# Global attention of a two-block transformer kernel: every unit in two halves with a lead of 13 steps, and three pieces of preparation moved

## The chip, the cores and the metric

One core of a Trainium2 chip runs the kernel. The metric is device time in microseconds (us). TensorE is called PE, VectorE DVE, ScalarE ACT, GpSimd POOL and SyncE SP; SP issues the DMAs.

## The reference

`x` has 2 batches of 2048 tokens with 256 channels, in float32. Two stages follow each other:

```python
x = x + layernorm(attn(layernorm(x)))   # 16 heads of 16, rotary, softmax over all 2048 keys, Wo, bo
x = x + layernorm(ffn(layernorm(x)))    # two layers, each:
#   x = x + local_attention(shift_token(x) @ wqkv) @ wo   (8 heads of 64, window 128, l2norm, xpos)
#   x = x + (a * gelu(g)) @ w2 + b2, with a, g = split(LN(shift_token(x)) @ w1 + b1)
```

The diff touches the first attention, called global here, and the loading of the first weights of the local one.

## The kernel before

**Stages.** Up to 82 us the first batch is normalized and its keys, values and the first queries are projected. From 82 to 1559 us runs the global attention, with the projections of the second batch beside it. After that come the two local layers, which the diff leaves as they are.

**Units and steps.** A unit is (batch, group of 4 heads, block of 512 queries): 32 units in that order. A unit has 16 steps; in each, PE makes 2048 columns of scores (`se`, L543: 50 rows, of which 48 hold three-way split keys and queries and two hold the negated row maximum in a high and a low part), ACT takes four exps of 128x512 (`pe`, L548), and PE multiplies the exps of the step before with the values (`pv`, L517). `spans(u)` cuts the first four units (`HALVED`) into two halves of 256 queries with 8 steps of two key tiles each; the others run whole. In a half, a step's scores are 8 matmuls of 128x256, in a whole unit 4 of 128x512. At the end of a span `collect` (L559 on) copies `pv` to `ov` on ACT and stores it, five DMAs.

**Maxima.** The exact row maximum of a later unit is computed ahead: `row_max` (L436) makes 4 score matmuls per step (`sm`, L412) and DVE reduces each (L452). Since the maximum must be in place before the unit's scores, `finish_max` (L469) follows when a span is complete: negate on DVE (`nm`, L472), split on POOL (`mp`, L477 and L478), then, `DELAY` = 4 steps later, a transpose on PE (`tn`, L481), a copy on ACT (`mt`, L485), a store to DRAM (`md`, L488) and four loads into the two extra rows of the queries (`qs<-md`, L491). The maxima run 13 steps ahead at the start; every fourth step makes two more, until the lead is `TAIL` = 26 steps. So the last 26 steps have no maxima; there the four PSUM banks of pool "sm" are dealt anew as two places of two banks, and the exps are 1024 wide.

**Side work.** `main_loop` writes the order of PE, DVE, ACT and POOL by hand: it takes steps (`s`) and maxima (`m`) in turn, and two lists of generators, `side` (projections of queries and of the second batch, then the closing of blocks: divide by the sums, multiply by Wo, normalize) and `early` (normalizing the second batch's blocks, rotary tables), each of which gives at most one piece in a step. `load_queries` (L398, from `qd` in DRAM) runs when the maxima come near a unit, `load_keys` (L385, from `kd`) one step into each group. `output_weights` (L805) is called at step 3. SP's queue isn't in the hand-written order: the scheduler places its DMAs by its own estimates. After the loop, `last_steps`, three blocks closed by `close_block` (L575) and the pieces left over are merged by their planned times with the local layers; the first local weights are loaded by a strand at -50, with their split on DVE behind the last maxima (L957).

```python
for strand in (s, m, m, s, s, m):   # one step: 3 s, 2 m ... and 2 s, 1 m after the side matmul
    next(strand, None)
if n % EVERY == 0 and lead < TAIL:
    for _ in range(2):
        next(maxima)
    lead += 0.5
side.step(PRODUCTS)
```

Of the kernel before, what the change touches and what calls it, by code (L numbers as in the profile page):

```python
# [20 lines left out]
P = 128  # L21
# [7 lines left out]
NG = 4  # L29
# [18 lines left out]
def tile_sandwich(  # L48
# [369 lines left out]
    def spans(u):  # L418
        return [(0, 2), (2, 4)] if u < HALVED else [(0, 4)]

    def first_max(k, pm):

        q, keys = qs[0], ks[0]
        n = 0
        for t in range(*spans(0)[0]):
            for j in range(0, 4, 2):
                for i in range(2):
                    sc = one("sm", "sm")
                    scores(q, keys, j + i, t, k, sc)
                    nc.vector.tensor_reduce(pm[:, t, j + i, k : k + 1], sc, AX.X, ALU.max)  # L430
                n += 1
                yield 1.2 * n


    reduced, unfinished = [], []

    def row_max():

        due = []
        for u, (b, g, k) in enumerate(units):  # L440
            q, keys = qs[u], ks[g % 2]
            for span in spans(u):
                if (u, span) == (0, spans(0)[0]):
                    continue
                pm = small.tile([P, 4, 4, NBLK], F32, tag="pm", name="pm", bufs=2)
                for t in range(*span):

                    for j, half in [(j, half) for j in (0, 2) for half in (0, 2)]:
                        for kk, i in ((half, 1), (half, 0), (half + 1, 1), (half + 1, 0)):
                            sc = one("sm", "sm")  # L450
                            scores(q, keys, j + i, t, kk, sc)
                            ins = nc.vector.tensor_reduce(  # L452
                                pm[:, t, j + i, kk : kk + 1], sc, AX.X, ALU.max
                            )
                            reduced[:] = [ins.ins]
                            if (kk, i) != (half + 1, 0):
                                yield
                        if (t, j, half) == (span[1] - 1, 2, 2):
                            due = [DELAY, finish_max(u, span, pm)]
                            next(due[1])  # L460
                            unfinished[:] = due[1:]
                        if due and due[0] == 0:
                            for _ in due[1]:
                                pass
                        if due:
                            due[0] -= 1
                        yield
# [32 lines left out]
    TAIL, HALVED, DELAY = 26, 4, 4  # L500


    IN_TURN = {1: (0, 1, 2, 3), 2: (0, 2, 1, 3)}

    def attend():
# [4 lines left out]
        def values(u, span, s, n, pe, pv):  # L510
            b, g, k = units[u]
            w = 512 // n
            for i in range(n):
                for j in range(4):
                    o = (s + i) * 272 + (4 * g + j) * (D1 + 1)
                    c = (4 * i + IN_TURN[n].index(j)) * w
                    nc.tensor.matmul(  # L517
                        pv[SL * j : SL * (j + 1), :w],
                        va[b][:, o : o + SL],
                        pe[c // 1024][:, c % 1024 : c % 1024 + w],  # L520
                        start=(s + i == 0),
                        stop=(s + i == NT - 1),
                    )
            if s + n == NT:
                collect(u, span, pv)

        waiting = None
        for u, (b, g, k) in enumerate(units):
            q, keys = qs[u], ks[g % 2]
            for span in spans(u):  # L530
# [3 lines left out]
                for s in range(0, NT, n):  # L534
                    pe = [t4("pe", tag="pe") for _ in range(2)]

                    m = 2 if u * NT + s >= len(units) * NT - TAIL else 1
                    for c in range(0, 2048, 512 * m):
                        sc = one("se") if m == 1 else two("se")
                        for o in range(c, c + 512 * m, w):  # L540
                            i, j = s + o // (4 * w), IN_TURN[n][o // w % 4]
# [14 lines left out]
                    if (u, s + n) == (len(units) - 1, NT):  # L556
                        values(*waiting)
# [61 lines left out]

    def close_in_pieces(b, k):  # L620
# [31 lines left out]
        for t in range(4):  # L652
            py = one("py", "sm")[:, :C]
# [6 lines left out]
            nc.scalar.copy(y[:, t, :], py)  # L660
            nc.gpsimd.tensor_tensor(y[:, t, :], y[:, t, :], bias_o[0], ALU.add)
# [38 lines left out]
    def first_block(k):  # L700
# [14 lines left out]
        parts0[k] = xh, xl, first_cs if k == 0 else rotary(k, "pe" if k < 2 else "t4")  # L715
# [51 lines left out]

    merged(in_order(strands))
    for _ in finish_max(0, spans(0)[0], pm0):
        pass  # L770
# [3 lines left out]
    lead, EVERY = 13, 4  # L774
    for _ in range(4 * (lead - 8)):
        next(maxima)
# [28 lines left out]
    def output_weights():  # L805
        raw = split_weights("o", wo1, nc.gpsimd, nc.gpsimd.tensor_copy)

        bo = sb.tile([P, C], F32, tag="bo", name="bo")
        bo_raw = t4("bo_raw")[:, :C]
        nc.sync.dma_start(bo_raw, bo1.partition_broadcast(P))  # L810
        bvs = t2("bvs").rearrange("p (c t) -> p c t", c=4)
        for c in range(2):
            nc.vector.tensor_copy(bvs[:, c, :], bqkv[:, 4 + c : 5 + c].to_broadcast([P, P]))
        pb = one("pb", "sm")
        for c in range(2):
            nc.tensor.matmul(pb[:, :C], bvs[:, c, :], raw[:, c, :], start=(c == 0), stop=(c == 1))
        nc.vector.tensor_tensor(bo, bo_raw, pb[:, :C], ALU.add)
        return bo
# [25 lines left out]
    def main_loop(lead, loaded):  # L844
        normalized = {}
        early = Pieces(
            *[normalized_block(1, k, normalized) for k in range(NBLK)],
            *[rotary_tables(l) for l in range(DEPTH)],
        )
        side = Pieces(  # L850
            *[project_qk(0, k, 0, *parts0[k]) for k in range(2, NBLK)],
            *[project(1, k, normalized) for k in range(NBLK)],
        )
        for n in range(1, len(units) * NT - TAIL + 1):
# [5 lines left out]
            if n % EVERY == 0 and lead < TAIL:  # L860
                for _ in range(2):
                    next(maxima)
                lead += 0.5
            side.step(PRODUCTS)
            for strand in (s, m, s):
                next(strand, None)
            early.step(OTHER, WAIT)
            side.step(OTHER, WAIT)
            if n % NT == 0:
                b, g, k = units[n // NT - 1]  # L870
                if g == NG - 1 and (b, k) < (1, 1):
                    side.add(close_in_pieces(b, k))
# [7 lines left out]
            if (n + lead + 3) // NT >= loaded and loaded < len(units):  # L880
                load_queries(loaded)
                loaded += 1
            if n == 3:
                bias_o.append(output_weights())
        assert next(maxima, 0) == 0 and early.kind is None
        return side

    in_turn = {mybir.EngineType.PE}
    with tc.manual_schedule(engines=ENGINES):
        side = main_loop(lead, loaded)  # L890
# [4 lines left out]
    def last_steps():  # L895
        for n in range(TAIL):
# [7 lines left out]
    strands = [(LAST - TAIL * STEP, last_steps())]  # L904
    for i, place in enumerate((LAST + CLOSE, LAST + CLOSE - NT * STEP, -46.0)):
        strands.append((place, close_block(B - 1, NBLK - 1 - i, "t4" if i > 0 else "pe")))

    def last_pieces():
        while side.kind is not None:
            side.step(PRODUCTS, OTHER, WAIT)  # L910
            yield 0.0

    strands.append((-50.0, last_pieces()))
# [8 lines left out]
    zero = sb.tile([1, C], F32, tag="zero", name="zero")  # L922
    mid_d = {
# [21 lines left out]

    def raw_columns(src, nk, n, step, tag):

        sv = src.rearrange("(k p) o -> p k o", p=P)
        for o in range(0, n, step):
            m = min(step, n - o)  # L950
            raw = t4("raw", tag=tag)[:, : nk * m].rearrange("p (k o) -> p k o", k=nk)
            nc.sync.dma_start(raw, sv[:, :, o : o + m])
            yield o, m, raw

    weights = {}

    def load_attn_weights(l, pace, tag, copy):  # L957
        tiles = [large_v(0, f"attnh_{l}", F32R), large(0, f"attnl_{l}", F32R)]
        n = 2 * 3 * INNER
        wq = [t[:, :n].rearrange("p (k o) -> p k o", k=2) for t in tiles]  # L960
        wo = [t[:, n : n + 4 * C].rearrange("p (k o) -> p k o", k=4) for t in tiles]
        weights["attn", l] = wq, wo
        if l == 0:
            nc.gpsimd.memset(zero, 0.0)
        t = 0.0

        for n in (1, 0, 2):
            cols = slice(n * INNER, (n + 1) * INNER)
            for _, _, raw in raw_columns(wqkv2[l][:, cols], 2, INNER, INNER, tag):
                yield t + 4.0  # L970
                with tc.issue_after(reduced[-1]):
                    split(wq[0][:, :, cols], wq[1][:, :, cols], raw, copy=copy)
                t += pace
                yield t
        for _, _, raw in raw_columns(wo2[l], 4, C, C, tag):
            yield t + 4.0
            with tc.issue_after(reduced[-1]):
                split(wo[0], wo[1], raw, copy=copy)
# [62 lines left out]
    WEIGHTS_FROM = -50.0  # L1041
# [496 lines left out]
    strands.append((WEIGHTS_FROM, load_attn_weights(0, 2.0, "t4", nc.vector.tensor_copy)))  # L1538
    ffn_weights_from = LAST + 20.0
    for l in range(DEPTH):  # L1540
# [14 lines left out]
        if l + 1 < DEPTH:  # L1555
            strands.append((start + 55.0, load_attn_weights(l + 1, 20.0, "pe", nc.scalar.copy)))
# [108 lines left out]
```

## Time and profile before

| | |
|---|---|
| runs | 2873.26, 2874.59, 2887.58 us; median 2874.59 |
| profiled run | 2879.28 us, of which the span is 2877.5 us |
| mean granted PE clock | 0.973 of full speed |
| busy: PE, DVE, ACT, POOL | 2707.5, 2317.9, 1898.2, 1288.1 us |
| DMA | 163.72 MB, 57 GB/s on the mean |

A line of the groups reads: line, engine, operation, out<-in, shape, count, then busy time and mean ns of one, then the idle time of the engine just before such instructions and what ended it. A line of a timeline reads: start, duration, engine, line, operation, count, and in brackets the idle time before it and its releaser. The chain of waits is followed back from the end; each piece has its start and its length. `PEclk` gives the granted clock in 40 slices of the span, in tenths; 9 is 90% or more.

### The profile page before, as it was taken

The page shows a single profiled execution, that of the slowest core. Times are in us where ns is not written, and L with a number is a line of the kernel's source. Part 1 is how long each engine was busy: PE and PEld are TensorE (multiplying, and loading weights), DVE is VectorE, ACT ScalarE, POOL GpSimd, SP SyncE. Part 2 cuts the span into 40 slices and gives each one's busy share as a digit, 9 for nine tenths or more (in the row PEclk, how much of TensorE's full clock was granted, in tenths as well). Part 3 has the DMA queues.
Part 4 walks back from the last instruction along what each step waited for, and adds up shares of the span by engine and source line. Part 5 has one row for each costly group of instructions (what it writes and reads, how often), then busy time and mean ns, then how long its engine had stood idle before and what let it go on. Part 6 is the DMA issues. An engine that isn't in the chain of part 4 may idle for free.

```text
span 2877.5 us, 50638 instructions
## 1 busy us (share of the span) xinstructions
PE 2707.5 (94%) x18496; PEld 1627.8 (57%) x18496; DVE 2317.9 (81%) x5006; ACT 1898.2 (66%) x4015; POOL 1288.1 (45%) x1244
## 2 busy tenths in 40 slices
PE   7989999999999999999988899999999899999998
PEld 5545433333333333333334777777788678787787
DVE  6878888889999999999975788887454788887565
ACT  3456677777878777788876576676443667676432
POOL 4253212131121312200036688886455678786465
PEclk8789999999999999999999999999999999999999
DMA  7033211111111111100022110111232111111232
GB/s 218 20 92 112 67 30 43 42 46 53 40 34 51 52 38 47 54 9 17 18 91 84 52 50 31 32 47 44 81 108 59 54 42 39 34 44 41 82 106 71
DMA packets 154721, 163.72 MB, mean 57 GB/s; under 512 B 32716, under 2 KB 117880, under 8 KB 154472
## 3 DMA queue, kind: packets, MB, share of 16 engines
q1 hardware_dynamic: 154472, 160.48, 18.7%
q8 instruction: 147, 2.41, 0.4%
q14 instruction: 102, 0.84, 0.1%
HBM read 98.89 MB, written 49.04 MB: 51 GB/s over the span
## 4 chain that ended last, share of the span: by engine, by line
PE 74%; DVE 11%; ACT 8%; POOL 3%; issue 2%; DMA 2%; SPq 0%; POOLq 0%; DVEq 0%; ACTq 0%
PE pv L517 17%; PE se L543 15%; ACT pe L548 5%; PE sm L412 4%; PE s L1240 4%; PE o L1307 3%; DVE pm L452 3%; PE w L1289 3%; PE p L172 3%; PE p L176 2%; PE p L174 2%; PE pag L172 2%; PE pag L174 2%; PE pag L176 2%; PE t L1214 2%
## 5 line engine op out<-in xcount | busy, mean ns | idle before, releaser
L452 DVE TENSOR_REDUCE pm<-sm 128x1 f32<-128x512 f32 x2016 | 1247.7, 683 | 119.9 <-PE sm L412 92.0
L548 ACT ACTIVATE pe<-se 128x512 f32<-128x512 f32 (+1 forms) x1996 | 1060.3, 614 | 349.1 <-PE sm L412 258.1
L412 PE MATMUL sm<-ks,qs 48*128 48x512 f32 x2048 | 778.0, 462 | 21.9 <-DMA qs<-qd 8.3
L543 PE MATMUL se<-qs,ks 50*128 50x512 f32 (+1 forms) x2304 | 743.1, 421 | 53.4 <-ACT pe L548 49.8
L543 PEld LDWEIGHTS se<-qs,ks 50*128 50x128 f32 x2304 | 361.3, 190 | 619.6 <-ACT pe L548 536.5
L517 PE MATMUL pv<-pe,va 128*32 128x512 f32 (+1 forms) x4608 | 557.3, 566 | 0.0
L412 PEld LDWEIGHTS sm<-ks,qs 48*128 48x128 f32 x2048 | 355.3, 190 | 62.2 <-DVE pm L452 32.2
L1279 POOL TENSOR_TENSOR e<-e,rs 128x1024 f32<-128x1024 f32 (+1 forms) x128 | 254.2, 1986 | 86.6 <-DVE rs L1275 86.6
L1264 ACT ACTIVATE e<-e,mns 128x256 f32<-128x256 f32 (+1 forms) x512 | 253.4, 498 | 15.4 <-DVE mns L1252 11.7
L477 POOL CAST mp<-nm 128x16 fp32r<-128x16 f32 (+1 forms) x35 | 6.9, 198 | 523.7 <-DVE nm L472 268.6
L95 POOL TENSOR_TENSOR rn<-ss,mhalf 128x8 f32<-128x8 f32 x128 | 214.9, 1679 | 10.6
L1166 ACT ACTIVATE sq<-p 128x512 f32<-128x512 f32 x128 | 76.6, 598 | 173.7 <-PE p L176 171.0
L1252 DVE CUSTOM_DVE_ANT_0 e<-s,mask 128x256 f32<-128x256 f32 (+1 forms) x512 | 181.5, 410 | 10.8 <-PE s L1240 9.4
L1189 POOL TENSOR_TENSOR ra<-qk,tab 128x512 f32<-128x512 f32 x128 | 171.8, 1354 | 18.2 <-DVE qk L1181 18.2
L517 PEld LDWEIGHTS pv<-pe,va 128*32 128x32 f32 x4608 | 99.0, 110 | 134.9 <-issue 107.9
L172 PE MATMUL p<-attnh,xTh 128*128 128x512 f32 x384 | 169.1, 440 | 2.9 <-ACT kT L1227 2.5
L1199 DVE TENSOR_TENSOR rb<-qk,tab 128x256 f32<-128x256 f32 x256 | 164.8, 684 | 0.4 <-PE pv L517 0.2
L1296 ACT COPY eT<-w 128x1024 f32<-128x1024 f32 (+1 forms) x128 | 126.0, 984 | 49.9 <-PE w L1289 47.9
L333 POOL TENSOR_TENSOR rotation<-raw,cs 128x512 f32<-128x512 f32 x40 | 50.4, 1282 | 232.7 <-ACT raw L329 232.7
L174 PE MATMUL p<-attnl,xTh 128*128 128x512 f32 x384 | 153.4, 400 | 0.0
L1240 PE MATMUL s<-kT,qT 64*128 64x256 f32 (+1 forms) x1024 | 142.8, 397 | 11.2 <-ACT qT L1224 3.1
L176 PE MATMUL p<-attnh,xTl 128*128 128x512 f32 x384 | 153.2, 399 | 0.0
(201 smaller groups left out, 4864.4 us busy)
## 6 DMA issues: line engine op xcount, KB each, us to landing
xb<-mid SPq DMA_DIRECT2D x32, 512.0 KB
qs<-qd SPq DMA_DIRECT2D x192, 64.0 KB
kd<-parts SPq DMA_DIRECT2D x16, 512.0 KB
ks<-kd SPq DMA_DIRECT2D x64, 128.0 KB
qd<-parts SPq DMA_DIRECT2D x16, 512.0 KB
tab<-rotary SPq DMA_DIRECT2D x64, 128.0 KB
mid<-xb SPq DMA_DIRECT2D x16, 512.0 KB
xt<-in_x SPq DMA_DIRECT2D x12, 512.0 KB
```

Source lines behind the costliest of these rows:

```text
L95: nc.gpsimd.tensor_tensor(dst, src, mhalf[:, :n], ALU.pow)
L172: nc.tensor.matmul(out, lh, rh, start=first, stop=False)
L174: nc.tensor.matmul(out, lh, rl, start=False, stop=False)
L176: nc.tensor.matmul(out, ll, rh, start=False, stop=last)
L412: return nc.tensor.matmul(out, q[rows, j // 2, t * P : (t + 1) * P], keys[rows, k, j // 2, :], start=True, stop=True)
L452: ins = nc.vector.tensor_reduce(pm[:, t, j + i, kk : kk + 1], sc, AX.X, ALU.max)
L517: nc.tensor.matmul(pv[SL * j : SL * (j + 1), :w], va[b][:, o : o + SL], pe[c // 1024][:, c % 1024 : c % 1024 + w], start=(s + i == 0), sto ...
L543: nc.tensor.matmul(sc[:, o - c : o - c + w], keys[rows, i // 4, j // 2, i % 4 * P : (i % 4 + 1) * P], q[rows, j // 2, span[0] * P : span[1 ...
L548: nc.scalar.activation(pe[c // 1024][:, c % 1024 : c % 1024 + 512 * m], sc, AF.Exp, scale=1.0 / math.sqrt(D1),)
L1240: nc.tensor.matmul(get(f"s{hf}", two)[:, o + lo : o + 2 * P], at["qT"][own, a * P : (a + 1) * P], kT[own, windows, a, :], start=True, stop ...
L1264: nc.scalar.activation(e4(h // 4)[:, h % 4, lo:], e4(h // 4)[:, h % 4, lo:], AF.Exp, bias=mns[:, h : h + 1], scale=-1.0, accum_out=rs[:, h ...
L1279: nc.gpsimd.tensor_tensor(e4(hf)[:, :, lo:], e4(hf)[:, :, lo:], rs[:, hs].rearrange("p (a o) -> p a o", o=1).to_broadcast([P, 4, 2 * P - lo]),
```

## The change

Every unit of the global attention is now cut in two halves (`SPANS`), so each runs 8-step halves, with the matmuls of 128x256 that the first four units had; transposes, negations and output copies rise from 36 to 64, the stores of maxima with them, and the loads of maxima from 144 to 256. The lead of the maxima is 13 steps throughout (`LEAD`); no extra maxima are made, the main loop has 499 steps for 486, and the tail 13 for 26. A strand `third_queries` projects the third block's queries ahead of the main loop. `output_weights` becomes a generator among the early pieces, with its copies on POOL and its loads ahead of four waits. The first local weights are loaded and split by POOL in pieces from step 452 on (`load_attn_weights` through `in_steps`), for DVE at the transition. Of the last batch's blocks, two (for three) are closed by `close_block`; the block (1, 1) is closed in pieces from a list of its own, `last`. `issue_after` and `reduced` are gone.

```diff
-    def spans(u):
-        return [(0, 2), (2, 4)] if u < HALVED else [(0, 4)]
+    SPANS = [(0, 2), (2, 4)]
...
-            for span in spans(u):
-                if (u, span) == (0, spans(0)[0]):
+            for span in SPANS:
+                if (u, span) == (0, SPANS[0]):
...
-    TAIL, HALVED, DELAY = 26, 4, 4
-    IN_TURN = {1: (0, 1, 2, 3), 2: (0, 2, 1, 3)}
+    LEAD, DELAY = 13, 4
+    IN_TURN = (0, 2, 1, 3)
...
-                    m = 2 if u * NT + s >= len(units) * NT - TAIL else 1
+                    m = 2 if 2 * u * NT + span[0] // 2 * NT + s >= 2 * (len(units) * NT - LEAD) else 1
...
+                            i, j = s + o // (4 * w), IN_TURN[o // w % 4]
...
-            py = one("py", "sm")[:, :C]
+            py = one("py", "sm" if "sm" in pools else "one")[:, :C]
+            live.append(py)
...
             nc.scalar.copy(y[:, t, :], py)
+            live.pop()
...
-        parts0[k] = xh, xl, first_cs if k == 0 else rotary(k, "pe" if k < 2 else "t4")
...
+    def third_queries():
+        n = 0.0
+        for kind in project_qk(0, 2, 0, *parts0[2]):
+            if kind == OTHER:
+                n += 1.0
+                yield n
+    strands.append((101.0, third_queries()))
...
-    lead, EVERY = 13, 4
-    for _ in range(4 * (lead - 8)):
+    for _ in range(4 * (LEAD - 8)):
...
     def output_weights():
-        raw = split_weights("o", wo1, nc.gpsimd, nc.gpsimd.tensor_copy)
+        t = t4("raw")
...
+        nc.sync.dma_start(bo_raw, bo1.partition_broadcast(P))
+        nc.sync.dma_start(raw, wo1.rearrange("(k p) o -> p k o", p=P))
+        for _ in range(4):
+            yield WAIT
...
+        split(*parts, raw, nc.gpsimd, nc.gpsimd.tensor_copy)
+        w1parts["o"] = parts
...
-        bo_raw = t4("bo_raw")[:, :C]
-        nc.sync.dma_start(bo_raw, bo1.partition_broadcast(P))
-        bvs = t2("bvs").rearrange("p (c t) -> p c t", c=4)
         for c in range(2):
-            nc.vector.tensor_copy(bvs[:, c, :], bqkv[:, 4 + c : 5 + c].to_broadcast([P, P]))
+            nc.gpsimd.tensor_copy(bvs[:, c, :], bqkv[:, 4 + c : 5 + c].to_broadcast([P, P]))
+        for _ in range(3):
+            yield WAIT
         pb = one("pb", "sm")
         for c in range(2):
             nc.tensor.matmul(pb[:, :C], bvs[:, c, :], raw[:, c, :], start=(c == 0), stop=(c == 1))
+        yield OTHER
         nc.vector.tensor_tensor(bo, bo_raw, pb[:, :C], ALU.add)
-        return bo
+        bias_o.append(bo)
...
+    def load_attn_weights(l, pace, tag, eng, copy):
...
+        for n in (1, 0, 2):
+            cols = slice(n * INNER, (n + 1) * INNER)
+            for _, _, raw in raw_columns(wqkv2[l][:, cols], 2, INNER, INNER, tag):
+                yield t + 4.0
+                split(wq[0][:, :, cols], wq[1][:, :, cols], raw, eng, copy)
+                t += pace
+                yield t
+        for _, _, raw in raw_columns(wo2[l], 4, C, C, tag):
+            yield t + 4.0
+            split(wo[0], wo[1], raw, eng, copy)
...
+    def in_steps(generator, waits):
+        for _ in generator:
+            for _ in range(waits):
+                yield WAIT
...
-    def main_loop(lead, loaded):
+    def main_loop(loaded):
         normalized = {}
         early = Pieces(
             *[normalized_block(1, k, normalized) for k in range(NBLK)],
+            output_weights(),
             *[rotary_tables(l) for l in range(DEPTH)],
         )
         side = Pieces(
-            *[project_qk(0, k, 0, *parts0[k]) for k in range(2, NBLK)],
+            project_qk(0, 3, 0, *parts0[3]),
             *[project(1, k, normalized) for k in range(NBLK)],
         )
-        for n in range(1, len(units) * NT - TAIL + 1):
+        last = Pieces()
+        for n in range(1, len(units) * NT - LEAD + 1):
             s, m = steps, maxima
             for strand in (s, m, m, s, s, m):
                 next(strand, None)
-            if n % EVERY == 0 and lead < TAIL:
-                for _ in range(2):
-                    next(maxima)
-                lead += 0.5
             side.step(PRODUCTS)
+            last.step(PRODUCTS)
             for strand in (s, m, s):
                 next(strand, None)
             early.step(OTHER, WAIT)
             side.step(OTHER, WAIT)
+            last.step(OTHER, WAIT)
             if n % NT == 0:
                 b, g, k = units[n // NT - 1]
-                if g == NG - 1 and (b, k) < (1, 1):
-                    side.add(close_in_pieces(b, k))
+                if g == NG - 1 and (b, k) < (1, 2):
+                    (side if (b, k) < (1, 1) else last).add(close_in_pieces(b, k))
             if n % (4 * NT) == 1 and n > 1:
                 i = n // (4 * NT) + 1
...
                     assert side.kind is None
                 if i < B * NG:
                     load_keys(i // NG, i % NG)
-            if (n + lead + 3) // NT >= loaded and loaded < len(units):
+            if (n + LEAD + 3) // NT >= loaded and loaded < len(units):
                 load_queries(loaded)
                 loaded += 1
-            if n == 3:
-                bias_o.append(output_weights())
+            if n == (len(units) - NBLK) * NT + 4:
+                early.add(
+                    in_steps(load_attn_weights(0, 0.0, "t4", nc.gpsimd, nc.gpsimd.tensor_copy), 2)
+                )
+        while live:
+            for pieces in (side, last):
+                if pieces.kind is not None:
+                    pieces.step(PRODUCTS, OTHER, WAIT)
         assert next(maxima, 0) == 0 and early.kind is None
-        return side
+        return side, last
...
     def last_steps():
-        for n in range(TAIL):
+        for n in range(LEAD):
...
-    strands = [(LAST - TAIL * STEP, last_steps())]
-    for i, place in enumerate((LAST + CLOSE, LAST + CLOSE - NT * STEP, -46.0)):
+    strands = [(LAST - LEAD * STEP, last_steps())]
+    for i, place in enumerate((LAST + CLOSE, LAST + CLOSE - NT * STEP)):
         strands.append((place, close_block(B - 1, NBLK - 1 - i, "t4" if i > 0 else "pe")))
-    def last_pieces():
-        while side.kind is not None:
-            side.step(PRODUCTS, OTHER, WAIT)
-            yield 0.0
-    strands.append((-50.0, last_pieces()))
+    def last_pieces(pieces):
+        n = 0.0
+        while pieces.kind is not None:
+            pieces.step(PRODUCTS, OTHER, WAIT)
+            n += STEP / 2
+            yield n
+    for pieces in left:
+        strands.append((LAST - LEAD * STEP, last_pieces(pieces)))
...
-    strands.append((WEIGHTS_FROM, load_attn_weights(0, 2.0, "t4", nc.vector.tensor_copy)))
```

## What is predicted

> **What bounds the kernel now.** I read the page first (span, busy shares, groups), then the timeline of ScalarE, because one step of the global attention is four exps of 128x512 and the time from the first exp of one step to that of the next is the price of a step; then the chain of waits around the odd steps; then SyncE's queue.
>
> ```profile
> span 2877.5 us, 50638 instructions
> ...
> PEclk8789999999999999999999999999999999999999
> ...
> L452 DVE TENSOR_REDUCE pm<-sm 128x1 f32<-128x512 f32 x2016 | 1247.7, 683 | 119.9 <-PE sm L412 92.0
> ...
> L543 PE MATMUL se<-qs,ks 50*128 50x512 f32 (+1 forms) x2304 | 743.1, 421 | 53.4 <-ACT pe L548 49.8
> ```
>
> PE is busy 94% of the span and hardly waits in the global attention, which the diff rewrites (82 to 1559 us; on every engine the instructions behind it stand in the same order in both kernels). A step also owes four row-max reduces, 4 x 0.683 = 2.73 us of VectorE, so VectorE is nearly as full as PE.
>
> ```profile
> 281.60 2.07 ACT L548 ACTIVATE pe<-se 128x512 f32<-128x512 f32 x4 [0.63 <-PE se L543]
> 284.36 2.06 ACT L548 ACTIVATE pe<-se 128x512 f32<-128x512 f32 x4 [0.70 <-PE se L543]
> 287.13 2.07 ACT L548 ACTIVATE pe<-se 128x512 f32<-128x512 f32 x4 [0.70 <-PE se L543]
> ...
> 289.90 1.57 ACT L548 ACTIVATE pe<-se 128x512 f32<-128x512 f32 x3 [0.44 <-PE se L543]
> ...
> 293.84 2.07 ACT L548 ACTIVATE pe<-se 128x512 f32<-128x512 f32 x4 [1.07 <-PE sm L412]
> ```
>
> Ordinary steps with a projection matmul take 2.77 us here (281.60 to 287.13 to 289.90); the step from 289.90 takes 3.94, since it carries the two extra maxima of every fourth step. The same view gives 2.69 for a halved step without projection (197.59 to 200.28) and 2.61 for a whole one (1303.72 to 1306.33). A transpose of maxima adds 0.43 to a step with a projection (499.20 to 502.40 is 3.20) and 0.21 to one without (2.82 against 2.61).
>
> Three steps are far off, where a load is late. Here the chain of waits around the third:
>
> ```profile
> 315.19 0.25 ACT mt L485
> 315.44 0.02 issue
> 315.45 3.62 DMA md<-mt
> 319.07 0.02 issue
> 319.09 0.02 SPq L491
> 319.11 0.03 issue
> 319.14 1.30 DMA qs<-md
> 320.44 0.14 issue
> 320.58 0.47 PE se L543
> ```
>
> PE stands for 2.22 us until the maxima are back from DRAM, and the table by windows shows what follows: the granted clock from 322 to 336 us is 0.51.
>
> ```profile
> 206.00:226.00 20.00, 19.84 (x114) 10.63 (x116) 10.31 (x16) 7.62 (x15) 6.78 (x8) 0.50 0.29 77
> 282.00:293.00 11.00, 10.79 (x112) 6.51 (x112) 10.16 (x18) 8.23 (x17) 1.40 (x3) 1.00 0.36 102
> 322.00:336.00 14.00, 14.00 (x60) 5.23 (x59) 7.45 (x12) 7.18 (x15) 1.96 (x2) 0.51 0.14 36
> ```
>
> The columns end with clock, DMA share and GB/s. At half clock a step takes 4.9 us instead of 2.77, so 43% of the throttled time is lost; the throttled stretches after stalls last 3.4 to 20 us, which makes 1.5 to 9 us each, 4.5 as a middle.
>
> **The change, part by part.** The sum is made against the profiled run, 2879.3 us (1.8 beyond its span, 4.7 above the median of the runs).
>
> *Lead constant, early steps (5 to 113; 369.7 us before).* The 26 extra pairs of maxima go: 1.2 to 1.45 us each, some 34 us. The three stalls as they stood go with their half clock: (11.13 - 2.77) + (8.5 and three of 4.9, less 4 x 2.77) + (6.4, 4.5, 4.9, 4.9, less 4 x 2.77), some 30. Built up afresh from the listing of the changed kernel's instructions: 90 steps with a projection at 2.77, 13 of those with a transpose at 3.20, 5 plain ones at 2.69 and one plain with a transpose at 2.90 make 307.3, which is **-62.4**.
>
> *Steps 114 to 193* (223.4 before): 58 x 2.77, 8 x 3.20, 12 x 2.69, 2 x 2.90 = 224.4, **+1.0**; the projections end earlier, but these units are halved now.
>
> *Steps 194 to 486* (782.5 before): 208 x 2.69, 29 x 2.90, 49 x 2.77, 7 x 3.20 = 801.7, **+19.2**. This is the price of halving where PE waits for ScalarE: the scores become 4096 matmuls of 128x256 for 512 and 1792 of 128x512, the first exp of a step needs two of them, and there are 28 more each of transposes, negated maxima and output copies. Bounds: +6, if each of the 38 halves there gets the 0.35 that a whole unit's switch saves (two steps in 2.69 + 2.18 for 5.22), or more if a matmul of 256 costs over half of one of 512. I take 19.2, from the halved steps that the trace has.
>
> *Third block's queries ahead:* 12 matmuls more before the loop, at half clock (55.9 to 103.7 us) some +2.6; the output-weight matmuls leave step 3, -2.0; fewer extra maxima there, -1.4: **-1**. *Weights in pieces on POOL:* POOL is 45% busy; casting and subtracting a 128x1024 piece, by the 1.28 us of its 128x512 products, is about 5 us, and POOL's other duty here, splitting the negated maxima (0.2 us), has four steps, 11 us, before the transpose. Hidden; if POOL were behind by more, each late transpose would cost what a late chain costs. *Last steps:* VectorE's casts leave steps 486 to 489, but 13 more steps keep their maxima: **+2.8** up to step 499, and **+2** for one more transpose and its copies in the 13 remaining steps (0 to 5).
>
> *The chain of maxima, now due at once.* In the trace, from the first exp of a step with a transpose to maxima landed takes 5.04 us: copy after the last exp, the store issued at about 2.2 us, its landing and the first load at 3.6, the loads 0.29 apart, 1.44 for the last transfers. Before, a lead that rises to 26 steps against units of 16 leaves 5 steps and more for it. In the new kernel half h begins two steps after its transpose, each time: the maxima are needed 5.37 us after that first exp beside projections (0.33 of slack) and 4.97 in plain steps, where the later loads miss their matmuls by about 0.43: 31 x 0.43 = **+13.3**. When a score matmul waits for it, the whole PE queue stands behind (maxima, values, projections), and with it the exps and reduces.
>
> A page speaks against the change here: the Trainium skill, "DMA: Bandwidth & Descriptors", in the section on what happens when a kernel issues a DMA, gives about 2.0 us fixed for each, most of it waiting for the write's receipt. By that, store and load would take 4.0 us for the measured 1.40 and 1.30 (501.36 to 502.76, and the chain above), every half would wait some 1.3 us longer, and the sum would be some 70 us higher; the trace has the shorter times, so they stand.
>
> So far -62.4 + 1.0 + 19.2 - 1 + 2.8 + 2 + 13.3 = -25, or 2854.
>
> *What is in SyncE's queue ahead of the chain.* The trace shows the chain late by 1 us and more for about a quarter of its 36 transposes, behind other traffic:
>
> ```profile
> 765.99 0.38 SPq L638 DMA_DIRECT2D rb<-rsum  x1
> 766.41 0.47 SPq L640 DMA_DIRECT2D xt<-in_x  x1
> 766.99 0.44 SPq L488 DMA_DIRECT2D md<-mt  x1
> 771.77 1.16 SPq L491 DMA_DIRECT2D qs<-md  x4
> ```
>
> Behind two loads of 512 KB the 16 KB store needs 4.78 us instead of 1.40. Before, nothing waited for it. The order of SyncE's queue is the scheduler's, and in the new kernel's listing these stand before the store, or between store and loads: both stores of the last queries at the third half (POOL issues the second 11.9 us after the projection's last step: late by 4.3); the rotary tables' 512 KB loads and the key reload around the sixth to ninth half (some 5); queries, keys and tables of the second batch at four halves (3.5 and 3 x 1.8); the closing of blocks (stores waiting for POOL's last add, the loads of sums, 5.0 us after their store, and key and weight loads) at halves 32 (2.3), 38 (5.9), 47 (weights, 2 MB at the 190 GB/s of the case above, 8), 48 (3.7), 59 (1.8) and 61 (3.3). Sum 43. Eight of these exceed 2.2 us, so the half clock may follow: 8 x 4.5 at 6 in 10, 22. Together **+65**, with 0 and 115 as ends: the scheduler's order is fixed, but whether the waits in it last is not known until it runs. That a stall costs its clock rests on the 2.22 us gap above.
>
> The Trainium skill, "TensorE: Matmul & The Clock Gate", "Why this matters for your kernels", would keep full speed up to gaps of about 3 us; by that, one of the eight (2.3) would go without its clock, 2.7 us less. The 2.22 us gap of this trace decides against it.
>
> 2854 + 65 = 2919 in the profiled run's terms, less 4.7: **2915**.
>
> **The rivals.** *First, faster:* the chain gets through in time, since the queue is in order but what stands ahead may be done by then. Price: the 65 is not paid, 2850. It decides at the store's landing: as long as the first load of maxima is issued within 3.9 us of the first exp of the transposing step, the 62 us stay gained. For it: three quarters of the chains of before were on time. Against it: those late ones were under lighter traffic (1079 transfers, now 1359). *Second, about the same:* only part of the delays occur, some 15 to 40 us, 2860 to 2889. *Third, much slower:* the early steps keep a hump (VectorE, at 2.73 of 2.77 us, doesn't catch up after a stall) or the reloads hold SyncE's queue longer than listed: the 34 us of maxima or 50 more of delays come back, 2960 and more. *Fourth, within the first:* halved plain steps take 2.61 like whole ones, 208 x 0.08 = 17 less: 2833.
>
> **How the numbers follow.** Forecast with its band 2889 to 2960: 0.48. First and fourth: 0.25. Second: 0.15. Third: 0.12. The range 2840 to 2970 leaves out the fourth and half of the third. 0.5%, 14 us, is about what a measurement can tell from no change, so faster is below 2860 and slower above 2889: 0.25, 0.15, 0.60. The forecast's own range is 2889 to 2960.
>
> **What would show it.** Right: steps of 2.77 without humps up to step 113; gaps on PE ended by the load of maxima at the named halves, with the clock at 0.5 behind some; halved plain steps at 2.69. Wrong: the chain's loads on time at all those halves (first rival), steps of 2.61 or of 2.8 and more in the late units, or POOL ending the wait for the transpose.

## The result, and the profile after

The changed kernel is slower: 2980.64 us in the median (2967.81 to 2989.69) for 2876.98, a ratio of 1.035 with an interval of 1.029 to 1.041. The forecast was 2915 with a range of 2840 to 2970: the right side, but the time lies above the range, and the loss is 104 us for a forecast 40. The profiled run took 2989.4 us, 110 more than that of the kernel before; times and stretches read from traces below are of the profiled runs.

The page of the changed kernel first: its span, the granted clock by fortieths, and the groups of the reduces and of the scores.

```profile
span 2987.6 us, 62908 instructions
...
PEclk8799899999999899999999999999999999999999
...
L451 DVE TENSOR_REDUCE pm<-sm 128x1 f32<-128x512 f32 x2016 | 1247.1, 681 | 255.8 <-PE sm L412 222.6
...
L541 PE MATMUL se<-qs,ks 50*128 50x256 f32 x4096 | 779.6, 314 | 137.4 <-DMA qs<-md 80.1
```

Two readings. The reduces cost what they did (1247 us), but VectorE now stands for 256 us before them, for 120 before. And the scores, which waited mostly for exps (49.8 of 53.4 us), now wait mostly for the load of the maxima. The view of the waits gives the number (us in total, times, longest):

```profile
PE se L541 <- DMA qs<-md: 80.1, 45, 9.5
PE se L541 <- ACT pe L546: 54.6, 207, 0.5
```

Seventeen of these waits are 1 us or longer and make 70 of the 80 us. The chain of waits around the second longest, before step 377 (dots stand for rows left out):

```profile
1245.34 1.68 SPq L848
...
1248.10 0.47 SPq L848
...
1248.67 6.67 DMA md<-mt
...
1255.40 1.27 DMA qs<-md
1256.68 0.14 issue
1256.81 1.08 PE se L541 x2
```

SyncE issues four 512 KB loads of the first local weights (L848), then the 8 KB store of the maxima (L486). ScalarE had copied the maxima by 1245.34; the store leaves at 1248.67, and 6.67 us later it has landed and the loads can go. PE stands for 8.6 us and then works at half clock, from 1251.72 to 1261.96: its two score matmuls of 256 columns take 1.08 us. Another place, by SyncE's timeline before step 65:

```profile
302.88 3.08 SPq L811 DMA_DIRECT2D rotary<-tab  x2
306.05 2.13 SPq L392 DMA_DIRECT2D ks<-kd  x4
308.28 0.37 SPq L486 DMA_DIRECT2D md<-mt  x1
311.14 1.14 SPq L489 DMA_DIRECT2D qs<-md  x4
```

Here the store has been ready since 299.7 and stands behind two stores of rotary tables that wait for POOL, and behind four key loads. The table by windows shows the clock after two of the waits (the last three columns are clock, DMA share and GB/s):

```profile
314.00:331.00 17.00, 17.00 (x101) 9.34 (x101) 9.77 (x17) 8.98 (x18) 3.82 (x6) 0.50 0.26 73
555.00:569.00 14.00, 13.86 (x88) 7.78 (x86) 7.97 (x14) 6.58 (x14) 0.40 (x2) 0.51 0.12 30
```

The first follows the wait of 9.5 us before step 65, the second one of only 2.35 us. Over the main loop (110 to 1597 us) the trace has 18 stretches at half clock of 3.4 to 27.3 us, 160 us in all.

By stretches of steps, from first exp to first exp, in us:

| steps | before | changed | lead 16, tables late (below) |
|---|---|---|---|
| start of step 1 | 82.1 | 86.1 | 84.3 |
| 1 to 4 | 26.0 | 23.9 | 27.7 |
| 5 to 113 | 369.7 | 352.9 | 312.1 |
| 114 to 193 | 223.4 | 245.5 | 224.5 |
| 194 to 486 | 782.5 | 871.6 | 797.9 |
| 487 to 510 | 69.0 | 81.0 | 72.2 |

### The profile page after: what moved, and what is told of

Read it like the earlier page. It is cut to its first block, busy times and chain, and to the rows that moved or that the text cites. A ratio compares the mean times of both kernels' runs of the same rounds, so it can differ in the third digit from the quotient of the medians.

```text
span 2987.6 us, 62908 instructions
## 1 busy us (share of the span) xinstructions
PE 2750.3 (92%) x23900; PEld 1932.4 (65%) x23900; DVE 2310.6 (77%) x5018; ACT 1905.7 (64%) x4099; POOL 1316.1 (44%) x1318
## 4 chain that ended last, share of the span: by engine, by line
PE 65%; DVE 10%; ACT 8%; DMA 7%; POOL 5%; issue 3%; SPq 1%; POOLq 0%; ACTq 0%; DVEq 0%
PE pv L515 14%; PE se L541 11%; PE sm L412 6%; ACT pe L546 5%; PE s L1273 3%; DVE pm L451 3%; PE o L1340 3%; PE w L1322 3%; PE p L172 3%; DMA md<-mt 3%; PE p L174 2%; PE p L176 2%; DMA qs<-md 2%; PE pag L172 2%; PE pag L174 2%
## 5 line engine op out<-in xcount | busy, mean ns | idle before, releaser
L541 PE MATMUL se<-qs,ks 50*128 50x256 f32 x4096 | 779.6, 314 | 137.4 <-DMA qs<-md 80.1
L541 PEld LDWEIGHTS se<-qs,ks 50*128 50x128 f32 x4096 | 525.1, 195 | 467.0 <-ACT pe L546 299.7
L515 PE MATMUL pv<-pe,va 128*32 128x256 f32 x8192 | 575.5, 400 | 1.0 <-ACT pe L546 0.3
L412 PEld LDWEIGHTS sm<-ks,qs 48*128 48x128 f32 x2048 | 392.6, 194 | 24.2 <-DVE pm L429 14.5
L475 POOL CAST mp<-nm 128x8 fp32r<-128x8 f32 x62 | 11.9, 193 | 783.5 <-DVE nm L470 678.4
L515 PEld LDWEIGHTS pv<-pe,va 128*32 128x32 f32 x8192 | 219.2, 112 | 176.5 <-issue 28.3
L1273 PE MATMUL s<-kT,qT 64*128 64x256 f32 (+1 forms) x1024 | 142.8, 397 | 10.2 <-ACT eT L1329 3.3
L1340 PE MATMUL o<-eT,v 128*64 128x128 f32 x1984 | 138.6, 282 | 12.1 <-ACT eT L1329 12.1
```

Source lines behind the costliest of these rows:

```text
L412: return nc.tensor.matmul(out, q[rows, j // 2, t * P : (t + 1) * P], keys[rows, k, j // 2, :], start=True, stop=True)
L515: nc.tensor.matmul(pv[SL * j : SL * (j + 1), :w], va[b][:, o : o + SL], pe[c // 1024][:, c % 1024 : c % 1024 + w], start=(s + i == 0), sto ...
L541: nc.tensor.matmul(sc[:, o - c : o - c + w], keys[rows, i // 4, j // 2, i % 4 * P : (i % 4 + 1) * P], q[rows, j // 2, span[0] * P : span[1 ...
L1273: nc.tensor.matmul(get(f"s{hf}", two)[:, o + lo : o + 2 * P], at["qT"][own, a * P : (a + 1) * P], kT[own, windows, a, :], start=True, stop ...
L1340: nc.tensor.matmul(ps("o")[D2 * par : D2 * par + D2, o : o + P], made[b, i - 1 + j]["v"][:, h * D2 : (h + 1) * D2], at[f"eT{hf}"][:, (2 * ...
```

## The experiments

Theory A: the sum without delays holds, and what was missing in it is the chain store, load of maxima, late behind SyncE's queue, with half clock after it. Theory B: halves are dear in themselves. Theory C: SyncE's many issues have become the bound. Ratios are to the kernel before, measured beside each.

**More slack for the chain.**

```diff
-    LEAD, DELAY = 13, 4
+    LEAD, DELAY = 16, 4
```

> The changed kernel with a lead of 16 steps for 13, so that the transpose of each half's maxima comes three steps (some 8 us) earlier against the half that needs it. Theory A (the chain store, load of maxima is late behind SyncE's queue, and half clock follows): the gaps on PE of 1 to 8.6 us that end with a load of maxima vanish, at most the two longest (9.5 and 8.6 us) leave 1 us or so, the clock stays at full speed in the main loop after step 5, and the time falls by 110 to 135 us, to 2845 to 2875. Theory B (halves themselves are dear: twice the matmuls, twice the transposes, more transfers): 2940 and more. Theory C (SyncE has become the bound by its number of issues): the late loads come back at other halves, 2920 and more.

Measured 2861.67, ratio 0.993 (0.990 to 0.995): 119 us less than the changed kernel by three steps of lead, with the same halves, transposes and transfers. One wait for maxima is left:

```profile
PE se L541 <- ACT pe L546: 61.6, 225, 0.6
PE tn L479 <- DVE pm L451: 7.9, 35, 0.7
PE se L541 <- DMA qs<-md: 6.0, 1, 6.0
```

B and C fall as causes of the loss: the halves and the number of transfers stay, the loss goes.

**One step of slack** (`LEAD` 14).

> The changed kernel with a lead of 14 for 13: one step (2.7 us) more for the chain. Theory A: each gap of the changed kernel that ended with a load of maxima is 2.7 us shorter or gone, so of 17 gaps over 1 us nine are left with some 34 us, and their half clock; with 2850 as the sum without delays, 2900 to 2930. Theory C (late loads reappear wherever the lead puts the halves): no such order, 2940 and more.

Measured 2888.72, ratio 1.0025 (1.000 to 1.005): below the range that A gave. Five waits with 25.4 us stay where subtraction had said nine with 34. Three of them shrank by 0 to 2 us (9.5, 8.4 and 6.2 us, for 9.5, 8.6 and 8.2 with a lead of 13), not by 2.7, while others of 6 to 7 us are gone whole. An earlier store may find another queue ahead of it; that wasn't shown here. One step undoes 92 of the 119 us.

**The transpose two steps earlier** (`DELAY` 2, `LEAD` 13).

> The changed kernel with 2 steps for 4 between the negation and the transpose of the maxima, the lead left at 13: the chain starts two steps (5.4 us) earlier. Theory A: the gaps shrink by about 5.4 us each, six of them are left with 0.7 to 4 us, the half clock goes in some ten places, and the time is 2875 to 2915. Theory B: 2950 and more. A second price could show: POOL, in its bursts of projection work, splits the negated maxima too late for the earlier transpose, and PE waits for the split in the first 190 steps.

Measured 2878.46, ratio 0.9975 (0.995 to 1.000). Three waits for maxima, 13.8 us, are left; the two long ones are shorter by 0.9 and 3.3 us, not by 5.4 (8.6 for 9.5 before step 65, 4.9 for 8.2 before step 353). The second price shows, though not where it was expected: the transpose waits for POOL's split three times, 4.77 us at 800 us and 1.28 at 1067, behind POOL's other work.

```profile
PE se L541 <- DMA qs<-md: 13.8, 3, 8.6
...
PE tn L479 <- POOL mp L476: 6.5, 3, 4.8
```

**Halving alone** (the kernel before with `HALVED` 30, the lead still rising to 26).

> The kernel before with all but the last two units in halves (HALVED 30 for 4), the lead still rising to 26: halving alone, with slack for the chain. Theory A: 8 to 25 us above the kernel before, 2885 to 2900, with no gap on PE that ends with a load of maxima but the one before step 65. Theory B: 2960 and more. If plain halved steps gained at the switch what whole ones do, the same time as before, 2877.

Measured 2903.46, ratio 1.0071 (1.005 to 1.009): some 20 us, which is the +1.0 and +19.2 of the prediction (steps 114 to 193 take 226.0, 194 to 486 take 801.2). In its trace no score waits for a load of maxima.

**The third block's queries ahead, alone.**

```diff
+    strands.append((101.0, third_queries()))
...
-            *[project_qk(0, k, 0, *parts0[k]) for k in range(2, NBLK)],
+            project_qk(0, 3, 0, *parts0[3]),
```

> The kernel before with the third block's queries projected ahead of the main loop and nothing else. Expected by the sum of the prediction: the gap of 5.5 us before step 19 goes with its half clock (8 to 10 us), the projection at half clock ahead of the loop costs 2.6, so 2867 to 2873. Rival: the gap only moves to the next queries that are loaded late, 2875 to 2880.

Measured 2870.46, ratio 0.996 (0.994 to 0.998), some 11 us less. The gaps before steps 19 and 33 are both gone; the one before step 65 is now 4.0 us.

**The store of maxima on ScalarE's queue.**

```diff
-        nc.sync.dma_start(md.rearrange("t j s q -> (t j s) q"), mt.bitcast(F32))
+        nc.scalar.dma_start(md.rearrange("t j s q -> (t j s) q"), mt.bitcast(F32))
```

> The changed kernel with the store of the maxima issued by ScalarE right behind its copy, the loads left on SyncE. If the place of the store in SyncE's queue makes the chain late, the halves whose store stood behind other transfers (steps 16, 64, 256, 384, 472) gain 2.4 to 4.6 us each, some 15 to 25 in all with their clock, and those whose loads stood behind (steps 304, 488) stay as they are: 2935 to 2965. If the traffic itself (2 MB of weights before step 376, 1 MB before 472) delays the small transfers, those two stay too: 2955 to 2980.

Measured 2958.29, ratio 1.0285 (1.025 to 1.032): 22 us less than the changed kernel, a time that lies in both ranges and so doesn't decide. Waits for maxima fall from 80.1 to 59.1 us. Those at steps 304 and 488 stay (6.2 to 6.3 and 6.1 to 5.9 us), as expected of halves whose loads stood behind. The waits at steps 16, 256, 384 and 472 are shorter by 1.4 to 1.7 us, less than the 2.4 to 4.6 expected; the one at 288 grows from 1.1 to 4.7; and ScalarE now stands for 5.9 us itself before step 65, with the store of the maxima in its queue. Order and traffic aren't told apart by it: before step 377, where the wait falls from 8.6 to 2.4 us, three of the four weight loads now follow the loads of maxima.

**Lead 16 with the rotary tables at step 200.**

```diff
+            if n == 200:
+                early.add(*[rotary_tables(l) for l in range(DEPTH)])
```

> The kernel with a lead of 16, and the rotary tables of the local layers put among the early pieces at step 200 for step 25 or so, when no projections are left. If the one gap that the lead of 16 has (6.0 us at 291 us, with 10.2 us at half clock) comes from the stores of those tables ahead of the key reload and the store of maxima in SyncE's queue, it goes: 8 to 11 us less than with the lead of 16 alone, 2850 to 2855 where that one has 2862. If the key reload itself makes the chain late, the gap stays: 2860.

Measured 2849.58, ratio 0.990 (0.987 to 0.993), some 28 us below the kernel before and the fastest of all: the gap at 291 us is gone, and no score waits for maxima at all.

**The same with a lead of 18.**

> The same with a lead of 18: two steps more of slack, 2 steps more of maxima before the loop and 2 fewer at the end. If the lead of 16 with the tables moved has no late chain, more slack brings nothing: within 4 us of it. If chains are still late there, another 3 to 8 us less.

Measured 2860.09, ratio 0.9935 (0.991 to 0.996): slower by 10, where 4 was the bound. No chain is late; what grows are steps 1 to 4 (32.8 for 27.7) and 487 to 510 (76.7 for 72.2). More slack than the chain needs costs.

**With a lead of 15.**

> The kernel with the rotary tables late and a lead of 15 for 16: one step less of maxima ahead of the loop, one step less of slack. If 8 us of slack are what the chain needs: one or two late chains come back, 2855 to 2870. If 5.4 us do now that the tables are out of the way: 2845 to 2851.

Measured 2878.73, ratio 0.998 (0.996 to 1.001), above both ranges. The two longest waits are 8.6 and 5.1 us. SyncE's timeline around the first:

```profile
735.28 1.36 SPq L796 DMA_DIRECT2D tab<-in_xpos_s  x1
746.03 0.37 SPq L811 DMA_DIRECT2D rotary<-tab  x1
746.49 0.52 SPq L486 DMA_DIRECT2D md<-mt  x1
749.41 1.15 SPq L489 DMA_DIRECT2D qs<-md  x4
```

The store of a rotary table waits for POOL until 746.03, and the maxima, copied since 734, behind it. With a lead of 16 the store of the same half leaves 0.5 us after its copy (720.15, copied at 719.66). So the order at one place decides, and one step of lead moves the order.

**The price of a stall by itself.** Spare copies on ScalarE ahead of one step in 16 halves of the kernel with lead 16 and the tables late, three in one kernel and six in the other.

```diff
+                    if 12 <= u < 28 and span == SPANS[0] and s == 8:
+                        for _ in range(3):      # 6 in the second
+                            nc.scalar.copy(pe[0][:, 0:512], va[b][:, 0:512])
```

> The kernel with a lead of 16 and the rotary tables late, which has no late chain, and on purpose three spare copies of 128x512 on ScalarE ahead of one step in the middle of 16 halves (units 12 to 27), some 1.6 us each time, so that PE stands for about 1.2 us with nothing else changed. If a short gap costs itself alone: 16 x 1.2 = 19 us or less, 2864 to 2870. If it is followed by half clock, as after the gaps of 1.0 to 1.7 us in the changed kernel: throttled stretches of 3.4 to 6.8 us after most of them, 1.5 to 3 us each more, 2885 to 2915.

> The same with six copies, some 3.2 us each time, so that PE stands for about 2.8 us. Gap alone: 16 x 2.8 = 45, 2890 to 2897. With half clock after each (7 to 10 us throttled, 43% of what of it PE works): 3 us or so more each, 2925 to 2955.

Measured 2908.62 (ratio 1.009, 1.006 to 1.012) and 2985.58 (1.033, 1.027 to 1.040): the first in its upper range, the second above both. These times don't decide, since late chains came back in both (two waits, 11.4 and 13.4 us, before steps 225 and 353 as with a lead of 15), in the first a gap of 9.0 us at 1554 too. The stalled halves themselves do. One of the 16 falls into a stretch that was at half clock already. At the other 15, with three copies, PE stands for 0.95 to 1.4 us, and 5 are followed by half clock, for 3.4 to 6.8 us; the 13 steps around a stall (the copies come in the fourth) are longer by 1.1 us or so than in the kernel without copies (but for one next to a late chain), and by 2.3 to 3.6 at four of the five; at the fifth the kernel without copies is at half clock itself. With six copies PE stands for 2.9 to 3.35 us, all 15 are followed by 3.4 to 17.1 us, and the 13 steps are longer by 7.6 us in the median (4.1 to 9.7). Copies, then the steps behind them, on ScalarE's timeline of the second:

```profile
1075.13 3.86 ACT L538 COPY pe<-va 128x512 f32<-128x512 f32 x6
1079.03 2.07 ACT L549 ACTIVATE pe<-se 128x512 f32<-128x512 f32 x4
1083.10 2.08 ACT L549 ACTIVATE pe<-se 128x512 f32<-128x512 f32 x4 [2.00 <-PE sm L412]
1087.23 2.08 ACT L549 ACTIVATE pe<-se 128x512 f32<-128x512 f32 x4 [2.06 <-PE sm L412]
1091.37 2.08 ACT L549 ACTIVATE pe<-se 128x512 f32<-128x512 f32 x4 [2.06 <-PE sm L412]
```

Steps of 2.68 us are 4.13 for as long as the clock is 0.50, as its table by windows says:

```profile
1073.00:1079.00 6.00, 3.07 (x35) 1.79 (x33) 4.37 (x7) 5.77 (x11) 0.00 (x0) 0.97 0.01 3
1079.00:1095.00 16.00, 15.32 (x106) 8.82 (x108) 10.39 (x22) 8.30 (x16) 0.63 (x3) 0.50 0.00 1
```

## Why the prediction was wrong in its size

**The sum without delays held within 10 us.** The kernel with lead 16 and the tables late is the changed kernel without its delays: steps 5 to 113 take 312.1 (forecast 307.3), 114 to 193 take 224.5 (224.4), 194 to 486 take 797.9 (801.7). Its profiled run is 2850.8 us; the forecast without delays was 2854 with the 13.3 us of waits in plain steps, which it doesn't have, so 2841 is what compares. Halving costs 20 us, as the kernel with 30 halved units shows, and the early gain was there to be had: steps 5 to 113 are 58 us shorter than before, 62 forecast.

**"Together +65" is the step that failed.** The changed kernel's profiled run less this one is 139 us, against 65 for the queue and 13.3 for the waits in plain steps. The mechanism was right; two terms were too small.

*The stalls:* 80 us for 43 + 13.3. The mechanism and most places were right: the waits at the places named, from the third half on, are 4.8, 1.1 and 9.5 (the rotary and key traffic, some 5 forecast), 2.4, 1.6 and 1.7, 3.7, 6.2, 8.6, 3.8, 7.3 (1.8 forecast) and 6.1 us (3.3 forecast), 57 in all. Not named were five halves with 12.9 us, 8.2 of it before step 353, where eight stores of outputs, whose place waits for POOL's product, stood ahead of the store of maxima:

```profile
1171.14 4.98 SPq L571 DMA_DIRECT2D oraw<-ov  x8
1176.22 0.52 SPq L486 DMA_DIRECT2D md<-mt  x1
```

The small waits of the other halves, 10 us, are the 13.3 of the plain steps. I priced each place by what was listed ahead of the store, and too low where that waited in turn: for POOL before step 65, for the stores of the inverted sums (`rsum`) before 473 and 489.

*The clock:* some 59 us (139 less 80) for 22. This is what is left over, not a measurement of its own. An estimate from the trace: PE works for 123 of the 160 us at half clock, and 35% (steps of 4.13 for 2.68 us) to 43% of them are lost, 43 to 53 us. The mean clock over the main loop, of the changed kernel and of lead 16 with the tables late:

```profile
110.00:1597.00 1487.00, 1343.79 (x14011) 814.45 (x14012) 1234.56 (x2107) 1056.76 (x2126) 318.19 (x409) 0.94 0.16 45
110.00:1490.00 1380.00, 1307.71 (x14386) 803.82 (x14386) 1255.41 (x2155) 1082.86 (x2173) 338.40 (x428) 1.00 0.18 50
```

The forecast gave half clock to eight stalls at 6 in 10, so some five stretches, and 4.5 us each. The price of one was not too low (59 over 18 is 3.3); their number was. In the trace 18 stretches followed, after waits of 1.0 to 1.7 us too, seven of which were each followed by 3.4 to 13.7 us. The spare copies agree in part: after 3.3 us always, after 1.4 us in 5 of 15. The choice to count only stalls above 2.2 us took the 2.22 us gap for the smallest that counts; the trace of before has PE stand for 1.59 us until 1484.78, and half clock from 1486.13 on.

The Trainium skill, "TensorE: Matmul & The Clock Gate", in "Why this matters for your kernels", asks for no gaps above about 3 us; here gaps of 1.0 to 1.7 us were followed by half clock, so the measurement decides: that limit did not protect this kernel.

The 2.0 us per DMA that the prediction set against its chain (the Trainium skill, "DMA: Bandwidth & Descriptors") stand in the section "Anatomy of one DMA — SWDGE (gpsimd) path", for DMAs issued by GpSimd. SyncE issues those of the maxima, and in the changed kernel their stores again took 1.4 us at most halves, from issue to the first load's, so that the prediction was right to go by the trace.

**The rivals.** The first (the chain in time) missed: three steps of lead make it true but for one wait (2862), and with the tables late wholly, at 2850 as priced. The second didn't occur. The third came true by its second half: SyncE's queue held the chain longer than listed, while the hump of VectorE that it also named isn't there (in the main loop the maxima's score matmuls have no wait for reduces in the changed kernel's list, 4.8 us before). The fourth missed by its condition, since a plain halved step takes 2.68 and not 2.61; but the switch saves all the same: between steps 194 and 486 step two of a half is about 2.25 long in 26 of 37 halves of the kernel without delays, which pays for the transposes.

**Single edits.** The third block's queries: 11 us gained alone, with the end of two of the three early stalls. Weights in pieces: POOL's work on them ends no wait for the transpose in the changed kernel, as forecast; but their loads, which I had listed, are the 8.6 us (8 forecast).

**What stays open.** The trace of the changed kernel divides the 17 waits in part. At eight of them the store left 0.9 to 8.6 us after ScalarE's copy, 34 us in all: that is its place in SyncE's queue. From the store's issue to the first load's went 1.4 to 6.7 us, some 29 us more in all than 17 times the 1.4 of a store with nothing ahead: the landing, and loads that stood behind other issues themselves. How much of a late landing is order in the DMA queue and how much the rate of the transfers ahead stays open, since moving the store moved both.

## What to carry to other kernels

When a change makes a chain through DRAM due at once, count the slack in steps first, then read what stands ahead of its transfers in the issuing queue, and what that waits for in turn; one step of slack was worth 92 us here, three 119, and two more than needed cost 10. A store that waits for a slow engine, issued on the same queue, stops everything behind it (9.3 us behind a rotary table's with a lead of 15). And price a stall of TensorE with its clock: a gap of 1.4 us cost 1.1, with half clock behind it 2.3 to 3.6; one of 3.3 us cost some 8.

## What was not expected of the hardware

Stretches at half clock come in multiples of 3.4 us (3.4, 6.8, 10.2, 13.7, 17.1), and begin within the gap or up to some 2 us behind it. In every trace here all changes of the clock lie on one grid of 3.41 us, and the place of a gap on this grid goes with what follows. Among the three spare copies, none of the six stalls that an edge of the grid cut in two was followed by half clock, and five of the nine that lay between two edges were; the seven of 1.0 to 1.7 us in the changed kernel all lay between two edges (to within 0.06 us), and all seven were followed. Why four of the nine weren't stays open. Nor is 1 us a limit below which nothing happens: in the kernel with lead 16 and the tables late, 6.8 us at half clock follow a wait of 0.72 us at 1137 us. And an 8 KB store behind 2 MB of loads took 6.67 us from issue to landing, for 1.4 with nothing ahead.
